# Modulated-convolution chain on one core: third output sum placed in PSUM, blurred taps built on TensorE, tap combinations and both ends reordered

## The chip, the cores and the metric

One core of a Trainium2 chip. The time is the device time of one execution in microseconds, data already in the chip's memory. Three runs of the kernel before took 515.73, 516.54 and 517.63 us; the median, 516.54 us, is the number to be compared. One further execution was taken with the hardware profiler; its own time is 515.94 us. All data are float32.

## The reference

Each of 128 samples has 64 channels and 1024 positions. A style vector of the sample gives each of four convolution layers a scale per input channel; the scaled weights are normalised per output channel; the four layers run one after the other and the input is added at the end:

```python
def _layer(x, style, w, b, mw, mb, typ):
    s = style @ mw.T + mb
    weight = SCALE * w * s[:, None, :, None]
    demod = lax.rsqrt(jnp.sum(weight * weight, axis=(2, 3)) + EPS)
    weight = weight * demod[:, :, None, None]
    ...                      # conv with 3 taps, + b
    # 'upsample': transposed conv of stride 2, then a blur (1,3,3,1)
    # 'downsample': the blur, then a conv of stride 2
...
for i, typ in enumerate(('same', 'upsample', 'same', 'downsample')):
    out = _layer(out, style, weights[i], biases[i], mod_w[i], mod_b[i], typ)
return x + out
```

There is no nonlinearity between the layers, so for each sample the whole chain is one filter of 9 taps of 64x64 matrices (different near the two ends of the sequence) and one constant per output channel.

## The kernel before, in words

**Filters.** Samples go in pairs (64 pairs p; one sample of the pair in partitions 0 to 63, one in 64 to 127) and the filters in quads of four samples (32 quads q, two pairs each). A quad's filter comes from three stages of matmuls, each followed by copies that multiply by a per-sample scale: `stage1` (matmuls L306, copies into S by L284 on ScalarE or L286 on VectorE), `stage2` (L337, copies into R), and `stage3` in two parts (L374, copies into Wf). `scale3` makes the scaled last-layer weights that stage 1 starts from. `stage2` multiplies S by E, the 9 taps of the upsampling layer with the two blurs already folded in (the seven factors of `BLUR2` over 3 taps). E is made once, near the start: VectorE clears it and `blur` adds seven scaled copies of the layer's weights (L275), in three portions that the written order spreads over the start. Then `residual` (L404) adds the input's own contribution to the centre tap, and `combine` (L412 to L416, five VectorE instructions of 384 columns) forms three sums of taps, H1, H2 and H3.

**Convolution.** The positions of a sample are split into three phases, positions 3j, 3j+1 and 3j+2, so that three outputs y0, y1, y2 of 170 columns each come from five products of filters of three taps instead of nine. The five inputs T of a pair are sums and differences of the phases: `pre1` makes G (L440, L443 on VectorE) and two of the five (L447, L448 on POOL), `pre2a` (L453) and `pre2b` (L463) the other three. `pre1` and `pre2a` also issue, on SP's queue, the loads of the pair four on. `convA12` computes the products with H1 and H2, `convA3` that with H3, into a PSUM tile psA; ScalarE copies m1 (L506) and m3 (L519, L520) to SBUF. `seed1` forms u and v (L528, L529), `seed2` adds u and m3 into Y (L547) and puts y1 = 2 m3 + v into SBUF (L548). Y is a PSUM tile of 512 columns for each of the pair's two samples, one bank each. `convB` accumulates the two last products onto Y's blocks 0 and 1 (matmuls at L481, as those of `convA`). `output` multiplies each sample's result by a scale and adds the constant: with ScalarE (L572) or VectorE (L574), one instruction of 340 columns from Y and one of 170 from y1. `store` sends the sample out, on SP's queue (L577). There is one Y for all pairs but a few at the end (`Y2`, two more banks, pairs 60 and 62).

**What sets the order.** Nothing is scheduled automatically: each engine executes its instructions in the order in which the program is written. The main loop, one pass for each quad, writes: stage 2 of quad q+2, `convB` and the outputs of pair 2q, stage 3 of quad q+2, `convA12` of pair 2q+2, inputs, stores, the seeds of pair 2q+1, `convA3`, then the same for pair 2q+1, stage 1 of quad q+3, and the combinations of quad q+2. Two tables put side work into it (`EXTRA` on VectorE and POOL, `SLOTS` on TensorE): constants, the normalisers of the later samples, and the few columns at both ends of the sequences. Samples are prepared in three parts (`PART`: 0 to 15, 16 to 31, the rest). The start (L816 to L898) is written out by hand: it computes the scales of part 0, makes the tables tA, tB, tC, t0, t3 that the stages multiply by, fills waiting time on TensorE with multiplications by zero (`zeros_to_y`), computes the constants of part 0 (`const_first`, `const_rest`; the last of them gives oc, which the outputs add) and works through quads 0 and 1 and pairs 0 to 2 until the loop can take over. `var_inverse`, `var_newton`, `table_A` and `table_C` turn a part's variances into its normalisers and tables, the first two on VectorE, the tables on POOL. The last two passes (q = 30, 31) have orders of their own; the last pair's outputs are written block by block, alternately on ScalarE and VectorE.

The code below has the line numbers of the profile.

## Time and profile before

| | |
|---|---|
| median of 3 runs | 516.54 us (515.73 to 517.63) |
| the profiled execution | 515.94 us |
| its span, first to last instruction | 514.1 us |
| TensorE, matmuls and weight loads | 492.9 us and 467.9 us busy (96% and 91%) |
| VectorE | 476.7 us (93%) |
| ScalarE | 364.0 us (71%) |
| POOL (GpSimd) | 159.7 us (31%) |
| mean granted clock of TensorE | 0.993 |
| DMA | 70.91 MB, 138 GB/s over the span |
| L547, the seed sum into Y | 62 times, mean 1083 ns |
| L548, y1 into SBUF | 64 times, mean 940 ns |
| L572, outputs on ScalarE | 340 columns and a few of 170: 126 times, mean 633 ns; 170 columns from y1: 125 times, mean 526 ns |

How the profile is read: PE is TensorE's matmuls and PEld its weight loads, which overlap; DVE is VectorE, ACT ScalarE, SP the engine whose queue issues loads and stores. A group of instructions is named by its line, its engine and what it writes and reads (`Y<-u,m` reads u and m and writes Y). Matmuls of 64x64 on different quarters of TensorE overlap (the 4608 of `convA` have a mean of 304 ns, and 193.9 us busy together), so a group's busy time is less than number times mean. A wait is written with the waiting instruction, then what released it (`PEld Y L481 <- DVE Y L547` is a weight load of `convB` that waited for the seed sum), the total in us, how often, and the longest. In rows in order of time, a bracket at the end holds the idle time before that instruction and what ended it.

### The profile page before, as it was taken

Reading aid. Unit: us, or ns where it says so; the run is one execution under the profiler, and the core shown is the slowest. Engines: PE = TensorE matmul, PEld = TensorE weight load, DVE = VectorE, ACT = ScalarE, POOL = GpSimd, SP = SyncE. Lnnn points to the kernel's source line nnn. Section 1 sums busy time; section 2 is a strip of 40 time slices with the busy share of each in tenths; the row PEclk is TensorE's granted clock in tenths of the full one; section 3 lists DMA queues with packets and bytes.
Section 4 is the critical chain, followed back from the end, with each engine's and each line's share of the span. In section 5 each row is a group of like instructions: output and inputs, shape, how many; then the busy total and the mean of one; then the engine's idle time right before and its main releaser. Section 6 shows DMA issues by size and latency. Waiting matters only on the chain.

```text
span 514.1 us, 28399 instructions
## 1 busy us (share of the span) xinstructions
PE 492.9 (96%) x12612; PEld 467.9 (91%) x12612; DVE 476.7 (93%) x869; ACT 364.0 (71%) x908; POOL 159.7 (31%) x196
## 2 busy tenths in 40 slices
PE   8998699998999999999999999999999999999994
PEld 5997699998899989999999999889999999999983
DVE  6899989999999999999989999989999979999994
ACT  3466567776766877777877777777777768777753
POOL 3315633443423331322221332331333213322210
PEclk9999999999999999999999999999999999999998
DMA  7125544553434544544554454554555435543223
GB/s 253 44 70 159 162 128 126 167 152 103 145 117 155 166 133 125 159 131 126 166 155 128 136 140 122 160 154 129 138 164 153 149 118 173 154 137 126 84 86 123
DMA packets 37162, 70.91 MB, mean 138 GB/s; under 512 B 4144, under 2 KB 28464, under 8 KB 37040
## 3 DMA queue, kind: packets, MB, share of 16 engines
q1 hardware_dynamic: 36960, 68.85, 44.3%
q8 instruction: 99, 1.62, 1.4%
q10 hardware_dynamic: 80, 0.25, 0.1%
q14 instruction: 23, 0.19, 0.1%
HBM read 35.46 MB, written 33.62 MB: 134 GB/s over the span
## 4 chain that ended last, share of the span: by engine, by line
PE 65%; DVE 20%; ACT 3%; issue 2%; DVEq 0%
PE psA L481 21%; PE Y L481 18%; PE psR L337 11%; PE psW L374 9%; PE psS L306 4%; DVE Y L547 3%; DVE T L463 3%; DVE y L548 2%; DVE G L440 2%; PE psE L724 2%; ACT o L572 2%; DVE G L443 1%; DVE u L528 1%; DVE T L453 1%; DVE H L413 1%
## 5 line engine op out<-in xcount | busy, mean ns | idle before, releaser
L481 PE MATMUL psA<-T,H 64*64 64x170 f32 x4608 | 193.9, 304 | 1.0 <-DVE v L529 1.0
L481 PEld LDWEIGHTS psA<-T,H 64*64 64x64 f32 x4608 | 176.9, 133 | 2.2 <-issue 1.6
L447 POOL TENSOR_TENSOR T<-G 128x342 f32<-128x342 f32 x62 | 57.0, 920 | 312.8 <-DVE G L443 266.7
L481 PE MATMUL Y<-T,Wf 64*64 64x170 f32 x3072 | 131.3, 307 | 12.0 <-DVE Y L547 10.9
L481 PEld LDWEIGHTS Y<-T,Wf 64*64 64x64 f32 x3072 | 115.9, 133 | 18.0 <-DVE Y L547 15.0
L572 ACT ACTIVATE o<-Y,oc,dm 128x340 f32<-128x340 f32 (+1 forms) x126 | 79.8, 633 | 48.0 <-PE Y L481 47.2
L374 PE MATMUL psW<-R,par_oi 64*64 64x256 f32 (+3 forms) x1536 | 92.4, 350 | 0.0
L284 ACT ACTIVATE Wf<-psW,t 128x256 f32<-128x256 f32 (+1 forms) x252 | 75.3, 381 | 22.5 <-PE psW L374 22.2
L337 PE MATMUL psR<-S,E 64*64 64x192 f32 (+1 forms) x2304 | 89.7, 299 | 0.2 <-ACT S L284 0.2
L547 DVE TENSOR_TENSOR Y<-u,m 128x680 f32<-128x680 f32 x62 | 67.2, 1083 | 17.2 <-ACT o L572 17.0
L337 PEld LDWEIGHTS psR<-S,E 64*64 64x64 f32 x2304 | 81.6, 133 | 1.7 <-ACT S L284 0.7
L448 POOL TENSOR_TENSOR T<-G 128x342 f32<-128x342 f32 x62 | 82.0, 1323 | 0.0
L374 PEld LDWEIGHTS psW<-R,par_oi 64*64 64x64 f32 x1536 | 73.2, 133 | 8.0 <-PE Y L643 0.3
L572 ACT ACTIVATE o<-y,oc,dm 128x170 f32<-128x170 f32 x125 | 65.8, 526 | 0.3 <-DVE y L548 0.3
L284 ACT ACTIVATE R<-psR,tC 128x448 f32<-128x448 f32 x63 | 36.5, 630 | 40.5 <-PE psR L337 40.5
L548 DVE SCALAR_TENSOR_TENSOR y<-m,v 128x340 f32<-128x340 f32 x64 | 60.2, 940 | 0.0
L440 DVE SCALAR_TENSOR_TENSOR G<-X 128x688 f32<-128x688 f32 x64 | 56.4, 882 | 0.0
L463 DVE TENSOR_TENSOR T<-G 128x684 f32<-128x684 f32 x64 | 56.3, 881 | 0.0
L306 PE MATMUL psS<-wd,par_oi 64*64 64x192 f32 x768 | 40.3, 324 | 0.0
L506 ACT ACTIVATE m<-psA 128x340 f32<-128x340 f32 x64 | 29.3, 458 | 10.4 <-PE psA L481 7.6
L306 PEld LDWEIGHTS psS<-wd,par_oi 64*64 64x64 f32 x768 | 32.2, 133 | 1.4 <-ACT wd L284 0.5
L528 DVE SCALAR_TENSOR_TENSOR u<-psA,m 128x340 f32<-128x340 f32 x64 | 32.1, 502 | 0.8 <-ACT m L520 0.8
(127 smaller groups left out, 446.1 us busy)
## 6 DMA issues: line engine op xcount, KB each, us to landing
out<-o SPq DMA_DIRECT2D x128, 255.0 KB, 3.6
X<-in_x SPq DMA_DIRECT2D x60, 344.0 KB, 3.2
X<-in_x SPq DMA_DIRECT2D x60, 172.0 KB, 3.5
X<-in_x SPq DMA_DIRECT2D x4, 516.0 KB, 6.5
Xe<-in_x_ends SPq DMA_DIRECT2D x1, 512.0 KB, 4.0
par_oi<-in_params_oi SPq DMA_DIRECT2D x2, 208.0 KB, 4.9
par_io<-in_params_io ACTq DMA_DIRECT2D x1, 240.0 KB, 3.8
par_io<-in_params_io SPq DMA_DIRECT2D x1, 240.0 KB, 4.4
```

The costliest lines, as they stand in the source:

```text
L284: nc_a.activation(dst, src, AF.Copy, scale=f)
L306: nc.tensor.matmul(ps[r][cols, k * C : (k + K) * C], woi[rows, 2, k, :], src[rows, :], start=(k == 0), stop=(k == K - 1), skip_group_check ...
L337: nc.tensor.matmul(ps[r][cols, lo * C : (lo + m) * C], E[rows, e + 2, :], src[rows, a, :], start=(n == 0), stop=(n == 8), skip_group_check ...
L374: nc.tensor.matmul(ps[r][cols, (lo - t_lo) * C : (hi - t_lo) * C], woi[rows, 0, k, :], rt[c][rows, lo - k : hi - k, :], start=(k == order[0]),
L440: nc_v.scalar_tensor_tensor(g[:, PL:], X[:, : 2 * PL], 0.5, X[:, PL:], op0=ALU.mult, op1=ALU.subtract)
L447: eng.tensor_add(t[:, 2, :NJ], plane(g, 2), plane(g, 1))
L448: eng.tensor_sub(t[:, 3, :NJ], plane(g, 2), plane(g, 1))
L463: nc_v.tensor_sub(t[:, 0:2, :NJ], both(a, PL), both(b, 1))
L481: nc.tensor.matmul(ps[s][cols], w, Ts[p][rows, SLOT[m], j : j + NB], start=(g == 0 and m not in (0, 4)), stop=(g == 2), skip_group_check=True,
L547: nc_v.tensor_add(blocks(Y), uu, m3)
L548: nc_v.scalar_tensor_tensor(y1, m3[:, :, 0, :], 2.0, v, op0=ALU.mult, op1=ALU.add)
L572: nc_a.activation(dst, src, AF.Identity, bias=add, scale=d3)
```

## The change

y1 is written into columns 340 to 509 of Y, beside the sums that `convB` accumulates on, and the output of a sample is one instruction of 510 columns from Y. E is made by TensorE: ScalarE makes four scaled copies of the layer's weights, 28 matmuls with the identity add them up in Y, one VectorE and one ScalarE copy bring them to E, whose taps are now stored even ones first. The combinations follow another order, with `residual` in their midst. At the start, the zero multiplications go partly to other banks; stage 1 of quad 0, the inputs of pair 0 (`pre1(0)`) and the last constant of part 0 come earlier, the normalisers of part 1 later, in the first pass of the loop behind the seeds of pair 1, and pair 0's stores both ahead of them. At the end, the pass q = 30 makes the last pair's inputs after the seeds of pair 61, its `convA3` right behind its `convA12`, and the first half of its seeds early; its outputs are all read from Y.

The diff; lines of code that only changed place are marked as removed and added.

```diff
     one = const.tile([P, 1], F32, name="one")
     eps = const.tile([P, 1], F32, name="eps")
     Z = const.tile([P, 512], F32, name="Z")
     E = const.tile([P, NT, C], F32, name="E")
+    w1s = const.tile([P, K + 1, K, C], F32, name="w1s")
     nc_v.memset(one, 1.0)
     nc_v.memset(Z, 0.0)
-    nc_v.memset(E, 0.0)
     nc_v.memset(eps, EPS)
 
     nc_a.activation(one, one, AF.Sqrt)
...
         table(nc_g, t3, bs, ALT, ODD, dm[:, 3, bs], var[:, 3, bs])
 
 
-    def blur(i, j):
-        for b in range(i, j):
-            dst = E[:, b : b + K, :]
-            nc_v.scalar_tensor_tensor(dst, w1r, BLUR2[b], dst, op0=ALU.mult, op1=ALU.add)
+    def blur_scale():
+        for i in range(K + 1):
+            nc_a.activation(w1s[:, i], w1r, AF.Copy, scale=BLUR2[i])
+
+    def blur_matmul(ps):
+
+        for b in range(len(BLUR2)):
+            w = w1s[:, min(b, len(BLUR2) - 1 - b)]
+            for r, rows in enumerate(HALF):
+
+                both = b % 2 == r
+                src = w[rows, 0::2] if both else w[rows, 1]
+                at = (b if both else b + 1) // 2
+                for cols in HALF:
+                    nc.tensor.matmul(
+                        ps[r][cols, C * at : C * (at + 1 + both)],
+                        idn[rows],
+                        src,
+                        start=(b == 0),
+                        stop=(b == len(BLUR2) - 1),
+                        skip_group_check=True,
+                    )
+
+    def blur_copy(ps, engs):
+        for r, (i, j) in enumerate(((0, 5), (5, NT))):
+            dst, src = E[:, i:j].rearrange("c e i -> c (e i)"), ps[r][:, : (j - i) * C]
+            if engs[r] is nc_a:
+                nc_a.copy(dst, src)
+            else:
+                engs[r].tensor_copy(dst, src)
 
 
     w3 = wio[:, 3]
...
                     src = st[c if r == 0 else 1 - c]
                     nc.tensor.matmul(
                         ps[r][cols, lo * C : (lo + m) * C],
-                        E[rows, e + 2, :],
+                        E[rows, e // 2 + 1 + (e % 2) * 5, :],
                         src[rows, a, :],
                         start=(n == 0),
                         stop=(n == 8),
...
         h1, h2, h3 = (H_[:, i] for i in range(3))
 
         nc_v.scalar_tensor_tensor(h2, c, -0.5, a, op0=ALU.mult, op1=ALU.add)
+        residual(q)
+        nc_v.scalar_tensor_tensor(h3, c, -1.5, h2, op0=ALU.mult, op1=ALU.add)
         nc_v.tensor_add(h1, h2, b)
         nc_v.tensor_sub(h2, h2, b)
-        nc_v.scalar_tensor_tensor(h3, c, -1.5, h2, op0=ALU.mult, op1=ALU.add)
-        nc_v.scalar_tensor_tensor(h3, b, 3.0, h3, op0=ALU.mult, op1=ALU.add)
+        nc_v.scalar_tensor_tensor(h3, b, 2.0, h3, op0=ALU.mult, op1=ALU.add)
 
 
     NJ = 2 * NB + 2
...
         nc_v.scalar_tensor_tensor(v, m2, 1.0 / 3.0, m1, op0=ALU.mult, op1=ALU.add)
         part[p] = m3, u, v
 
-    y1s = {}
-
     def seed2(p):
         if p >= NP:
             return
         m3, u, v = part.pop(p)
-        y1s[p] = y1 = m_tile("y1", p)
         uu = u[:, :, None, :].to_broadcast([P, 2, 2, NB])
         blocks = lambda y: y[..., : 2 * NB].rearrange("c s (i j) -> c s i j", i=2)
+        y1 = slice(2 * NB, 3 * NB)
         if p in Y2:
-            for s in range(2):
-                nc_v.tensor_add(
-                    blocks(y_bank(p, s)[:, None, :]), uu[:, s : s + 1], m3[:, s : s + 1]
-                )
+            ys = [(y_bank(p, s)[:, None, :], slice(s, s + 1)) for s in range(2)]
         else:
-            nc_v.tensor_add(blocks(Y), uu, m3)
-        nc_v.scalar_tensor_tensor(y1, m3[:, :, 0, :], 2.0, v, op0=ALU.mult, op1=ALU.add)
+            ys = [(Y, slice(0, 2))]
+        for y, k in ys:
+            nc_v.tensor_add(blocks(y), uu[:, k], m3[:, k])
+        for y, k in ys:
+            nc_v.scalar_tensor_tensor(
+                y[..., y1], m3[:, k, 0, :], 2.0, v[:, k], op0=ALU.mult, op1=ALU.add
+            )
 
     def seed(p):
         seed1(p)
...
         Ts.pop(p)
         os[p] = opool.tile([P, 2, HO], F32, tag="o", name=f"o{p}")
 
-    def output(p, s, eng=nc_a, parts=((0, 2), (2, 3))):
+    def output(p, s, eng=nc_a, parts=((0, 3),)):
 
         b = 2 * p + s
         d3, add = dm[:, 3, b : b + 1], oc[:, b : b + 1]
         for i, j in parts:
             dst = os[p][:, s, i * NB : j * NB]
-            src = y1s[p][:, s] if i == 2 else y_bank(p, s)[:, i * NB : j * NB]
+            src = y_bank(p, s)[:, i * NB : j * NB]
             if eng is nc_a:
                 nc_a.activation(dst, src, AF.Identity, bias=add, scale=d3)
             else:
...
     pm = [unit(ps_conv, f"psM{i}") for i in range(2)]
     BOTH = nc_a, nc_v
     LATER = slice(PART[0].stop, B)
+    Y2["fill"] = unit(ps_w, "psF")
     n_later = NL * (B - PART[0].stop)
     zeros_to_y(2, 512)
     nc_v.tensor_scalar_mul(mbs, mb, SCALE)
     mod_matmul(PART[0], pm[0][0])
     nc_a.activation(wsq[T, :2], wio[T, :2], AF.Square)
     nc_v.tensor_mul(wsq[T, 2:], wio[T, 2:], wio[T, 2:])
+    blur_scale()
     zeros_to_y(4, 256)
     mod_scale(PART[0], pm[0][0])
     nc_v.tensor_add(q2[T], wsq[T, :, 0, :], wsq[T, :, 1, :])
...
     for table_of in (table_B, table_0, table_02):
         table_of(PART[0])
     var_matmul(PART[0], pm[0][1])
-    blur(0, 1)
     var_root(PART[0], pm[0][1])
+    psB = [Y[:, r] for r in range(2)]
+    blur_matmul(psB)
     mod_matmul(LATER, pm[1][0])
 
-    zeros_to_y(4, 256)
+    zeros_to_y(2, 256, "fill")
     weight_sums()
     first_inverse(PART[0])
     table_A(PART[0], d2)
     scale3(0, BOTH)
+    blur_copy(psB, BOTH)
+    stage1(0, None, BOTH)
     scale3(1)
     nc_a.copy(raw[0][:, 0, :n_later], pm[1][0][:, :n_later])
-    blur(1, 3)
     var_inverse(PART[0])
     var_newton(PART[0])
     for of in (table_C, vector_c0, table_3, vector_a1, vector_Da, vector_b1, vector_c2):
         of(PART[0])
-    stage1(0, None, BOTH)
     scale3(2)
     zeros_to_y(2, 256)
-    blur(3, 7)
+    pre1(0, nc_v)
     mod_scale(PART[1], raw[0][:, 0], LATER)
     for of in (table_B, vector_a1, table_0, table_02, vector_b1, vector_c2):
         of(PART[1])
     stage2(0, None, BOTH)
-    pre1(0, nc_v)
     pre2a(0)
     zeros_to_y(2, 512)
     const_first(0, PART[0])
...
     stage3(0, 1, None, BOTH)
     stage1(2, ps_conv)
     const_first(2, PART[0])
-    residual(0)
     combine(0)
+    const_rest(2, PART[0], const_of(2, PART[0]))
     stage2(1, ps_conv)
     convA12(0)
     convA3(0)
...
     convA12(1)
     stage3(1, 1)
     convA3(1)
-    const_rest(2, PART[0], const_of(2, PART[0]))
-    residual(1)
     combine(1)
     pre2a(2)
     seed1(1)
     pre2b(1)
     pre1(3)
-    var_inverse(PART[1])
-    var_newton(PART[1])
-    table_A(PART[1], dm[:, 2, PART[1]])
-    for of in (table_C, vector_c0, table_3, vector_Da):
-        of(PART[1])
 
 
     REST = PART[2]
...
         if c < NQ:
             stage3(c, 0)
         if q == NQ - 1:
-            seed(p + 1)
+            seed2(p + 1)
         output(p, 1, nc_a if q < NQ - 1 else nc_v)
         if q == NQ - 1:
             store(p, 0)
...
         convA12(p + 2)
 
         if q:
-            pre2(p + 3)
+            if q < NQ - 2:
+                pre2(p + 3)
             store(p, 0)
             pre1(p + 4)
             store(p, 1)
             seed(p + 1)
+            if q == NQ - 2:
+                pre2(p + 3)
         else:
             store(p, 0)
+            store(p, 1)
             seed2(p + 1)
+            var_inverse(PART[1])
+            var_newton(PART[1])
+            table_A(PART[1], dm[:, 2, PART[1]])
+            for of in (table_C, vector_c0, table_3, vector_Da):
+                of(PART[1])
             pre2(p + 3)
-            store(p, 1)
             pre2b(p + 2)
             pre1(p + 4)
         EXTRA.get((q, 0), lambda: None)()
...
         convA3(p + 2)
         if q == NQ - 2:
             convA12(p + 3)
+            convA3(p + 3)
         side = SLOTS.get(q)
         convB(p + 1, (lambda: slot(*side)) if side else None)
         if q == NQ - 2:
             seed(p + 2)
+            seed1(p + 3)
         output(p + 1, 0)
         output(p + 1, 1, nc_a if q < NQ - 2 else nc_v)
         if c == NQ - 1:
...
         if s + 1 < NQ:
             scale3(s + 1)
         if c < NQ:
-            residual(c)
-            combine(c)
+                combine(c)
         EXTRA.get((q, 1), lambda: None)()
         if q < NQ - 2:
             convA12(p + 3)
-        convA3(p + 3)
+            convA3(p + 3)
 
 
 def kernel(x, cond_512, L0_cond_weights, L0_cond_biases, L0_cond_mod_w, L0_cond_mod_b):
```

## The prediction

> **What bounds the kernel now.** I read the page first, then the waits, then the timeline pair by pair. Engines first (busy us, share of the span, instructions):
>
> ```profile
> span 514.1 us, 28399 instructions
> PE 492.9 (96%) x12612; PEld 467.9 (91%) x12612; DVE 476.7 (93%) x869; ACT 364.0 (71%) x908; POOL 159.7 (31%) x196
> ```
>
> TensorE and VectorE are both nearly full, so neither share says which sets the end. The waits do (us in total, times, longest):
>
> ```profile
> DVE Y L547 <- ACT o L572: 17.0, 19, 3.0
> PEld Y L481 <- DVE Y L547: 15.0, 14, 3.1
> ...
> PE Y L481 <- DVE Y L547: 10.9, 10, 2.8
> ```
>
> The bound alternates. In some pairs `convB` waits for VectorE's seed L547 (VectorE leads); in others L547 waits for ScalarE's outputs, which follow TensorE (TensorE leads). Going through the 64 pairs in the timeline, VectorE leads in pairs 1 to 3, 6 to 19, 22 to 25, 32 to 39, and briefly at 43 and 53; TensorE in the rest. Pair 35, led by VectorE (start us, us):
>
> ```profile
> 306.32 0.92 POOL L447 TENSOR_TENSOR T<-G 128x342 f32<-128x342 f32 x1 [6.19 <-DVE G L443]
> ...
> 306.91 1.06 DVE L547 TENSOR_TENSOR Y<-u,m 128x680 f32<-128x680 f32 x1
> 307.19 1.54 POOL L448 TENSOR_TENSOR T<-G 128x342 f32<-128x342 f32 x1
> ...
> 307.88 1.22 DVE L548 SCALAR_TENSOR_TENSOR y<-m,v 128x340 f32<-128x340 f32 x1
> 308.02 1.65 PEld L481 LDWEIGHTS Y<-T,Wf 64*64 64x64 f32 x48 [0.75 <-DVE Y L547]
> ```
>
> TensorE starts 0.05 us after L547 ends (307.97), while L548 (y1) still runs: y1 is off TensorE's path today. L548 takes 1.22 us here and 0.50 elsewhere: L448 holds it up until 308.73, and 0.4 later it ends.
>
> **y1 to PSUM.** The instruction stays, one L548 per pair. No row shows this form writing PSUM; L547 (680 elements to PSUM) and L463 (684 to SBUF) both take 0.86 us undisturbed, so I take no change. Bounds 0 and +0.1 us each: it now waits for the instruction just ahead of it, which elsewhere costs VectorE 0.11 us; where L448 is in the way, that is hidden.
>
> Does its collision with POOL go, now that it no longer writes SBUF? The row first: L548 loses 0.72 us beside L448, while L528 and L529 lose nothing beside L447 (0.50 us); those read one operand from PSUM. The Trainium skill (SBUF — State Buffer, "SBUF: two separate sides") says that a VectorE instruction with two SBUF inputs and a GpSimd instruction that reads SBUF shut each other out for the whole instruction. It names inputs, not the output, and y1's inputs m3 and v stay in SBUF. If the write mattered, some 40 contended L548 would shed 0.72 us each, 29 us of VectorE time; by the rule nothing. I take nothing.
>
> What changes is who waits. y1 now lies in the bank that `convB` accumulates in. The row above says that `convB` needs L547 alone: cost 0. The Trainium skill (PSUM — Partial Sum Buffer, "PSUM bank collisions raise a hardware error") says that two engines may not touch one bank and quadrant together even at different columns, so waits go by bank. The built program does that: in every pair the first `convB` matmul waits for the y1 instruction instead of the seed sum. By the row 0; by the rule 1.08 us (y1's end less today's start) where VectorE leads. I take the rule. Queued behind that matmul on TensorE are the rest of `convB` and stages 1 to 3; ScalarE's outputs and the next L547 wait for those. For a pair's second `convB` y1 ends 0.7 to 2 us before TensorE comes: nothing there.
>
> Within a VectorE-led stretch this is a shift, not a sum. At pair 11 the outputs free Y at 128.88 and the next L547 starts at 129.97: 1.09 us of cover. One output of 510 columns replaces 340 and 170: ScalarE's rows from 64 to 448 columns rise 0.82 ns per column (315 to 630 ns), so 636+140=776 ns, 0.67 from start to start against 0.96 for the two; Y frees 0.15 us sooner. So the cover just holds. But each handover from VectorE to TensorE pays 1.08-0.15 once; without the cover, every pair of a stretch would pay it.
>
> **Combinations reordered.** One block today:
>
> ```profile
> 300.42 0.47 DVE L404 SCALAR_TENSOR_TENSOR Wf<-par_oi,t,Wf 128x64 f32<-128x64 f32 x2
> 300.81 0.54 DVE L412 SCALAR_TENSOR_TENSOR H<-Wf 128x384 f32<-128x384 f32 x1
> 301.39 0.56 DVE L413 TENSOR_TENSOR H<-H,Wf 128x384 f32<-128x384 f32 x1
> ...
> 303.17 0.56 DVE L416 SCALAR_TENSOR_TENSOR H<-Wf,H 128x384 f32<-128x384 f32 x1
> 303.65 0.51 DVE L453 TENSOR_TENSOR T<-X 128x342 f32<-128x342 f32 x1
> ```
>
> Each of the five steps needs the one before: 0.59 from start to start; the independent L453 follows after 0.48. Today 3.23 us. After, one dependent neighbour is left: four at 0.48, one at 0.59, two residuals at 0.2: 2.91. That saves 0.32 us per two pairs, on the path only where VectorE leads: seven times in pairs 6 to 19. h1 comes 0.4 us later; `convA12` comes 1.6 us after it, which covers that.
>
> **Start.** Off VectorE: the memset of E (0.48) and seven blur steps (7 x 0.36=2.5). Onto it: one PSUM copy (256 columns; L286 has 0.54 for 320: 0.45). Onto ScalarE: four copies of 192 (0.38 each, in its 2.4 us wait for the variance matmuls) and one of 320 (0.53). Onto TensorE: 28 short matmuls ahead of stage 1, for 4 zero matmuls less: 0 to 0.7 us, I take 0.3. VectorE is idle 3.5 us between 5 and 25, so the 2.5 are not simply won. And `pre1(0)` (2.2 us, 15.76 to 17.96) now stands ahead of VectorE's half of R: S ends at 12.0, Newton 1.3, `pre1(0)` 2.2, sc and ssq 0.5: R at 16.0+0.3, not 15.15. Stage 3 begins 1.2 later; behind it the waits for constants (0.41+0.34) go, as VectorE is ready then: +0.5 at the first u (28.05).
>
> From u on VectorE is full to pair 2 (51.71). The oc instructions leave this stretch (1.03 us, 31.31 to 32.34), combine(1) saves 0.3 but waits 0.5 for Wf: 0.5-1.0-0.3+0.5=-0.3. The inverses of part 1 (2.7 us, 39.68 to 42.38) move behind the second seed: `convB(1)`, which waits 2.12 us today, starts some 1.2 earlier, but those 2.7 us then stand ahead of pair 2, whose L547 gains 0.3 only. With y1, `convB(2)` is 0.8 later, `convB(3)` 0.5. POOL's tables follow the inverses later, and their readers (quad 4 on) come later still. SP's queue takes pair 0's second store ahead of two loads; they feed pairs four on. Behind pair 3 the clock matters (columns: width, busy us of PE, PEld, DVE, ACT, POOL; granted clock; DMA):
>
> ```profile
> 60.00:62.00 2.00, 0.00 (x0) 0.00 (x0) 2.00 (x5) 0.95 (x3) 1.29 (x2) 1.00 0.98 290
> 62.00:64.00 2.00, 1.59 (x30) 1.54 (x32) 2.00 (x4) 0.00 (x0) 1.93 (x3) 0.76 0.71 213
> 64.00:66.00 2.00, 2.00 (x34) 2.00 (x34) 2.00 (x4) 0.55 (x2) 1.92 (x3) 0.50 0.35 92
> 66.00:68.00 2.00, 2.00 (x54) 2.00 (x50) 1.21 (x3) 1.12 (x3) 1.08 (x3) 0.89 0.25 96
> ```
>
> After some 3 us without matmuls the clock halves for 3.4 us: 1.7 us lost, where TensorE leads. In the new order it is idle about 3.3 us before `convB(2)`, where VectorE's lead hides a slow clock, and 2.7 before `convB(3)`. Bounds 0 and -1.7; I take half, -0.85. At pair 5: -0.4.
>
> **Middle.** Pairs 6 to 19: 1.08-7x0.32-0.15=-1.3. Pairs 22 to 25, two savings only: +0.6. Pairs 32 to 39, with four and their own slack: 0. At 43 and 53: +0.6 and +0.4. In ten first halves led by TensorE y1 (0.50) ends 0 to 0.4 after `convB` starts today; POOL, released earlier, gives some back: +0.7. Sum +1.0.
>
> **End.** seed(61) now precedes pre2(63), so `convA12(63)` loses its 0.99 us wait, but its `convA3`, drawn ahead, waits 0.5 for m1's copy: the last matmul ends 0.5 sooner. Then:
>
> ```profile
> 508.06 0.49 ACT L572 ACTIVATE o<-Y,oc,dm 128x170 f32<-128x170 f32 x1 [1.19 <-PE Y L481]
> 508.59 0.45 DVE L574 TENSOR_SCALAR o<-Y,dm,oc 128x170 f32<-128x170 f32 x1 [1.18 <-ACT o L572]
> 509.08 0.49 ACT L572 ACTIVATE o<-Y,oc,dm 128x170 f32<-128x170 f32 x1 [0.52 <-DVE o L574]
> 509.60 0.45 DVE L574 TENSOR_SCALAR o<-Y,dm,oc 128x170 f32<-128x170 f32 x1 [0.56 <-ACT o L572]
> ```
>
> Four outputs, 0.51 apart, follow the last matmul in turn. The third block came from SBUF during `convB`; now it is in Y and joins them: six in turn, +1.0. End +0.5.
>
> **Sum.** -0.4+1.0+0.5=+1.1. The profiled execution took 515.94 us (514.1 span, 1.8 around it): 517.0. The median of the runs is 0.6 above it: 517.6.
>
> **Rivals.** (1) Slower: the wait for y1 is not won back. `convB` behind y1 at the ends of five VectorE-led stretches, 5 x 0.93=4.7, and 0.5 at the end: 521.7. For it: the built waits, and TensorE's start 0.05 after L547. It decides if the reorder saves under some 0.15 us per block; against that, 0.11 us per dependent step in the rows. (2) Faster: VectorE's relief reaches the end. 16 blocks at 0.32 are 5.1, within the 10.9 us that TensorE waits, and if y1 slips from behind POOL (0.50) the new wait is free: 511.4. For it: pairs 26 to 31, where y1 has 0.50. Against: in VectorE-led pairs POOL starts right after L443. (3) The start keeps the 2.5 us that leave VectorE, and the clock stays full: 513.0. Against: `pre1(0)` ahead of R.
>
> **How the numbers follow.** Near the old time 0.5; rival 1 0.3; rival 2 0.12; rival 3 0.08. A measurement of this kernel tells about 0.5% (2.6 us) from no change. The first case's own range is 515 to 520.5; 0.05 of it lies above 519.1, and half of rival 3 within the bound. Faster 0.17, same 0.49, slower 0.34. The range 512.6 to 522 cuts rival 2 and the tail of rival 1.
>
> **What would show it.** `convB`'s waits name y1; y1's median stays near 1.2 us; the block takes 2.9 us; outputs of 510 columns 0.78 us; six outputs in turn at the end; stage 3 of quad 0 about 1 us later. The forecast is wrong if y1 falls to 0.5 us throughout, if the clock drops in more places, or if the seeds no longer wait for outputs anywhere.

## The result, and the profile after

The changed kernel takes 525.46 us (four runs, 523.97 to 526.51) against 517.09 us for the kernel before (four runs, 515.73 to 518.06): 1.0162 times as long, 95% interval 1.0126 to 1.0197. The forecast was 517.6, with a range up to 522.0. The profiled execution took 525.72 us with a span of 523.9, against 514.1.

The page after, its first lines and the groups that answer to those of before (busy us, mean ns, then idle time before them and its releaser):

```profile
span 523.9 us, 28402 instructions
...
PE 499.4 (95%) x12660; PEld 471.0 (90%) x12660; DVE 458.5 (88%) x862; ACT 332.1 (63%) x789; POOL 150.0 (29%) x196
...
L509 PE MATMUL Y<-T,Wf 64*64 64x170 f32 x3072 | 129.8, 308 | 14.3 <-DVE Y L574 11.3
...
L600 ACT ACTIVATE o<-Y,oc,dm 128x510 f32<-128x510 f32 (+1 forms) x127 | 95.0, 773 | 54.1 <-PE Y L509 51.1
L572 DVE TENSOR_TENSOR Y<-u,m 128x680 f32<-128x680 f32 (+1 forms) x66 | 72.3, 1099 | 38.9 <-ACT o L600 38.7
...
L574 DVE SCALAR_TENSOR_TENSOR Y<-m,v 128x340 f32<-128x340 f32 (+1 forms) x66 | 45.4, 690 | 2.1
```

VectorE's busy time fell from 476.7 to 458.5 us and ScalarE's from 364.0 to 332.1, and the kernel became slower: less work, more waiting. The waits (us in total, times, longest):

```profile
DVE Y L572 <- ACT o L600: 38.7, 39, 3.2
...
PE Y L509 <- DVE Y L574: 11.3, 11, 3.6
...
PEld Y L509 <- DVE Y L574: 4.3, 2, 4.0
```

VectorE's seed sum now waits for ScalarE's outputs for 38.7 us in 39 places, not 17.0 in 19. Where `convB` waits for VectorE, it waits for y1 (L574), not for the sum, as forecast. (The profile puts another 10.9 us of waits ahead of `convB` down to ScalarE's copies into Wf. In the first halves looked at below those copies aren't what releases it: `convB` begins between 0.07 and 0.66 us after the last of them that had ended, but 0.14 or 0.15 us after y1 in every case.)

The chain behind this is seen in the timeline. This is the first half of one pass in which VectorE has slack, from the first `convB` to the second (start us, us, engine, line, what it writes and reads, count; in brackets the idle time before it and what ended it):

```profile
460.09 1.95 PE L509 MATMUL Y<-T,Wf 64*64 64x170 f32 x48
...
461.82 1.51 PE L401 MATMUL psW<-R,par_oi 64*64 64x320 f32 x24
462.10 0.78 ACT L600 ACTIVATE o<-Y,oc,dm 128x510 f32<-128x510 f32 x1 [0.60 <-PE Y L509]
...
463.36 1.25 ACT L311 ACTIVATE Wf<-psW,t 128x256 f32<-128x256 f32 x4 [0.48 <-PE psW L401]
...
464.11 0.93 POOL L476 TENSOR_TENSOR T<-G 128x342 f32<-128x342 f32 x1
464.48 0.79 ACT L600 ACTIVATE o<-Y,oc,dm 128x510 f32<-128x510 f32 x1
...
465.31 0.88 DVE L572 TENSOR_TENSOR Y<-u,m 128x680 f32<-128x680 f32 x1 [1.40 <-ACT o L600]
...
465.82 1.08 PE L509 MATMUL psA<-T,H 64*64 64x170 f32 x24
...
466.22 0.52 DVE L574 SCALAR_TENSOR_TENSOR Y<-m,v 128x340 f32<-128x340 f32 x1
...
466.89 1.39 PE L509 MATMUL Y<-T,Wf 64*64 64x170 f32 x32
```

Read it by who waits. ScalarE's first output (462.10) follows `convB`; then, by the written order, come stage 3's four copies (463.36), which wait for stage 3's matmuls; only then the second sample's output (464.48). It frees Y at 465.27, 5.18 us after `convB` began. The sum starts at 465.31, y1 behind it, and y1 ends at 466.74, 6.65 us after. The second `convB` begins at 466.89, 6.80 after. TensorE's own work between the two takes 6.59 us, as other runs below show. So even in this quiet pass the chain is 0.2 us too long; 0.15 of it is the longer output (y1_odd below, which has outputs of 340 and 170 columns again ahead of this sum, has 6.65 us here instead of 6.80). In a pass with side work on VectorE, POOL comes later and stands beside the sum:

```profile
325.26 0.80 ACT L600 ACTIVATE o<-Y,oc,dm 128x510 f32<-128x510 f32 x1
...
325.91 0.91 POOL L476 TENSOR_TENSOR T<-G 128x342 f32<-128x342 f32 x1
...
326.08 1.47 DVE L572 TENSOR_TENSOR Y<-u,m 128x680 f32<-128x680 f32 x1 [0.38 <-ACT o L600]
...
327.59 0.52 DVE L574 SCALAR_TENSOR_TENSOR Y<-m,v 128x340 f32<-128x340 f32 x1
```

Here the sum takes 1.47 us instead of 0.88, beside L476 on POOL, and the chain grows by as much: from `convB` at 320.87 to the next at 328.25 are 7.38 us. Such passes carry most of the loss. Against y1_sbuf (below; y1 in SBUF, the rest as in the change), the 25 first halves of q = 4 to 28 are 8.6 us longer together. Eight of them, in which the sum or y1 runs longer beside POOL, make 5.3 of that, at 0.3 to 0.9 each; fifteen make 3.3, at 0.2 to 0.3 each; two, led by VectorE in both kernels, lose nothing.

With all kernels of the study side by side (from their profiled executions; pass by pass for q = 4 to 28), the loss in the main loop lies in these first halves and nowhere else. What each kernel changes is told below; the columns from the fourth on are in us, but for the count:

| kernel | median us | ratio to before (95%) | `convB` of pair 5 begins | pair 5 to pair 59 | first half, mean | of 25 first halves below 6.62 us | second half, mean |
|---|---|---|---|---|---|---|---|
| before | 517.09 | | 79.2 | 408.6 | 6.93 | 11 | 8.26 |
| the change | 525.46 | 1.0162 (1.0126 to 1.0197) | 82.2 | 413.9 | 7.09 | 0 | 8.26 |
| y1_only | 532.22 | 1.0285 (1.0252 to 1.0318) | 82.2 | 418.7 | 7.28 | 0 | 8.26 |
| y1_sbuf | 511.63 | 0.9899 (0.9869 to 0.9929) | 79.3 | 404.2 | 6.75 | 16 | 8.25 |
| comb_only | 510.50 | 0.9880 (0.9851 to 0.9909) | 81.4 | 403.4 | 6.73 | 16 | 8.25 |
| old_start | 523.42 | 1.0131 (1.0099 to 1.0164) | 79.8 | 413.9 | 7.09 | 0 | 8.25 |
| out_early | 517.06 | 0.9988 (0.9975 to 1.0001) | 80.6 | 407.3 | 6.86 | 12 | 8.25 |
| out_early_sbuf | 519.55 | 1.0037 (1.0023 to 1.0050) | 78.9 | 412.4 | 7.05 | 0 | 8.25 |
| y1_first_sbuf | 513.75 | 0.9914 (0.9894 to 0.9933) | 81.3 | 405.2 | 6.79 | 16 | 8.25 |
| sbuf_oldblur | 512.20 | 0.9887 (0.9870 to 0.9905) | 81.1 | 404.2 | 6.75 | 16 | 8.25 |
| y1_even | 512.61 | 0.9913 (0.9889 to 0.9938) | 81.1 | 403.9 | 6.73 | 16 | 8.26 |
| y1_odd | 523.63 | 1.0113 (1.0076 to 1.0150) | 83.7 | 411.1 | 7.00 | 0 | 8.25 |
| comb_q0 | 508.73 | 0.9836 (0.9812 to 0.9860) | 77.3 | 404.1 | 6.75 | 17 | 8.25 |
| comb_q0_blur | 510.29 | 0.9865 (0.9813 to 0.9916) | 79.7 | 403.9 | 6.75 | 16 | 8.25 |

### The profile page after: what moved, and what is told of

The parts are those of the page before. It is cut to its first block, busy times and chain, and to the rows that moved or that the text cites. A ratio compares the mean times of both kernels' runs of the same rounds, so it can differ in the third digit from the quotient of the medians.

```text
span 523.9 us, 28402 instructions
## 1 busy us (share of the span) xinstructions
PE 499.4 (95%) x12660; PEld 471.0 (90%) x12660; DVE 458.5 (88%) x862; ACT 332.1 (63%) x789; POOL 150.0 (29%) x196
## 4 chain that ended last, share of the span: by engine, by line
PE 74%; DVE 11%; ACT 4%; issue 1%; DVEq 0%
PE psA L509 24%; PE Y L509 21%; PE psR L364 12%; PE psW L401 10%; PE psS L333 5%; DVE Y L572 3%; PE psE L752 2%; ACT Wf L311 2%; DVE Y L574 2%; ACT o L600 1%; DVE T L491 1%; DVE G L468 1%; DVE G L471 1%; DVE o L602 0%; DVE u L556 0%
## 5 line engine op out<-in xcount | busy, mean ns | idle before, releaser
L509 PE MATMUL psA<-T,H 64*64 64x170 f32 x4608 | 190.1, 304 | 0.7 <-ACT m L534 0.6
L509 PEld LDWEIGHTS psA<-T,H 64*64 64x64 f32 x4608 | 173.4, 133 | 1.7 <-ACT m L534 0.9
L475 POOL TENSOR_TENSOR T<-G 128x342 f32<-128x342 f32 x62 | 57.1, 920 | 325.7 <-DVE G L471 265.0
L509 PE MATMUL Y<-T,Wf 64*64 64x170 f32 x3072 | 129.8, 308 | 14.3 <-DVE Y L574 11.3
L509 PEld LDWEIGHTS Y<-T,Wf 64*64 64x64 f32 x3072 | 113.6, 134 | 24.6 <-ACT Wf L311 10.9
L600 ACT ACTIVATE o<-Y,oc,dm 128x510 f32<-128x510 f32 (+1 forms) x127 | 95.0, 773 | 54.1 <-PE Y L509 51.1
L572 DVE TENSOR_TENSOR Y<-u,m 128x680 f32<-128x680 f32 (+1 forms) x66 | 72.3, 1099 | 38.9 <-ACT o L600 38.7
L401 PE MATMUL psW<-R,par_oi 64*64 64x256 f32 (+3 forms) x1536 | 90.1, 350 | 0.2 <-DVE R L313 0.2
L476 POOL TENSOR_TENSOR T<-G 128x342 f32<-128x342 f32 x62 | 70.8, 1142 | 0.0
L574 DVE SCALAR_TENSOR_TENSOR Y<-m,v 128x340 f32<-128x340 f32 (+1 forms) x66 | 45.4, 690 | 2.1
L311 ACT ACTIVATE S<-psS,tB 128x320 f32<-128x320 f32 x63 | 29.8, 530 | 5.3 <-PE psS L333 3.9
```

Of the source, the lines that this page charges most:

```text
L311: nc_a.activation(dst, src, AF.Copy, scale=f)
L401: nc.tensor.matmul(ps[r][cols, (lo - t_lo) * C : (hi - t_lo) * C], woi[rows, 0, k, :], rt[c][rows, lo - k : hi - k, :], start=(k == order[0]),
L475: eng.tensor_add(t[:, 2, :NJ], plane(g, 2), plane(g, 1))
L476: eng.tensor_sub(t[:, 3, :NJ], plane(g, 2), plane(g, 1))
L509: nc.tensor.matmul(ps[s][cols], w, Ts[p][rows, SLOT[m], j : j + NB], start=(g == 0 and m not in (0, 4)), stop=(g == 2), skip_group_check=True,
L572: nc_v.tensor_add(blocks(y), uu[:, k], m3[:, k])
```

## The experiments

**y1 in PSUM alone, and undone.** Into the kernel before went only the changed `seed2` and `output`:

```diff
-        nc_v.scalar_tensor_tensor(y1, m3[:, :, 0, :], 2.0, v, op0=ALU.mult, op1=ALU.add)
+        for y, k in ys:
+            nc_v.scalar_tensor_tensor(
+                y[..., y1], m3[:, k, 0, :], 2.0, v[:, k], op0=ALU.mult, op1=ALU.add
+            )
...
-    def output(p, s, eng=nc_a, parts=((0, 2), (2, 3))):
+    def output(p, s, eng=nc_a, parts=((0, 3),)):
```

> The kernel before with one part alone: y1 goes to PSUM and each sample's output is one instruction (third block from Y at the end too). Theory 1 (one Y, a longer chain from one convB to the next): in TensorE-led passes convA3 of the first half is followed by convB after 1.06 us, not 0.87, in others after up to 1.8; passes 12 to 30 lose some 5 us, the VectorE-led passes before them some 2 more since the reordered combinations don't help here, the tail loses 1.0: 523 to 525 us. Theory 2 (y1 in PSUM is harmless, the middle loses by the reordered combinations and by collisions with POOL): at most 519 us.

It took 532.22 us, worse than either theory said. (In this kernel, and in old_start below, y1 of pair 0 overwrites the columns of Y from which the last constant of the first 16 samples is read afterwards, so that constant isn't the reference's; the instructions are the same.) The same edit reversed in the changed kernel:

> The changed kernel with that part undone: y1 in SBUF again, two outputs for each sample. Theory 1: the step from convA3 to convB is 0.87 us again in TensorE-led passes, 5 us come back in the middle and 1.0 in the tail: 519 to 520 us, 2.7 of the rest from the start. Theory 2: no more than 2 us come back, 523 us or more.

It took 511.63 us, faster than the kernel before. So y1 in PSUM costs 13.8 us (525.46 less 511.63) beside the reordered combinations, and 15.1 (532.22 less 517.09) without them. By place, from the profiles of the change and of y1_sbuf, which lie 14.9 us apart: 2.9 us before pair 5, 9.7 from there to pair 59, 2.3 behind it. (Of the 2.9, 1.3 lie ahead of pair 0's `convB`, where the two kernels do the same: that is a difference between two executions, see the start below.) Theory 2 falls. That more came than theory 1 said has one reason: I had read the cost off the change against the kernel before, where the gain of another part hid it.

**The combinations alone.**

```diff
-        nc_v.tensor_add(h1, h2, b)
-        nc_v.tensor_sub(h2, h2, b)
-        nc_v.scalar_tensor_tensor(h3, c, -1.5, h2, op0=ALU.mult, op1=ALU.add)
-        nc_v.scalar_tensor_tensor(h3, b, 3.0, h3, op0=ALU.mult, op1=ALU.add)
+        residual(q)
+        nc_v.scalar_tensor_tensor(h3, c, -1.5, h2, op0=ALU.mult, op1=ALU.add)
+        nc_v.tensor_add(h1, h2, b)
+        nc_v.tensor_sub(h2, h2, b)
+        nc_v.scalar_tensor_tensor(h3, b, 2.0, h3, op0=ALU.mult, op1=ALU.add)
```

> The kernel before with the reordered combinations alone. Theory 1: 0.3 us saved on VectorE in each block; it reaches the end where VectorE leads, about eight blocks, 1 to 2.5 us: 514.5 to 516 us. Theory 2 (h1 and h3 come later, TensorE waits for them): 518 us or more.

510.50 us: 6.6 us gained, more than twice what was expected. The block went from 3.23 to 2.85 us from start to start, in 30 blocks. First halves at TensorE's own pace, 6.59 us, are 16 of 25 instead of 11: VectorE's lead, which came and went in the kernel before, is gone in five more of them, and the others are shorter too (the 25 together by 5.0 us).

**Where y1's cost sits: the second output ahead of stage 3.** If the chain is what costs, it must help to let ScalarE free Y before stage 3's copies:

```diff
         output(p, 0)
+        if q < NQ - 1:
+            output(p, 1)
         if c < NQ:
             stage3(c, 0)
...
-        output(p, 1, nc_a if q < NQ - 1 else nc_v)
```

> The changed kernel with one edit: in the first half of a pass the second sample's output is written ahead of stage 3, so that ScalarE frees Y before it scales stage 3's first part, not after. Theory 1 (the cost of y1 in PSUM is the length of the chain convB, stage 3's copies, second output, seed sum, y1, next convB): the chain is 1.1 us shorter, below TensorE's own 6.6 us; convA3 is followed by convB after 0.87 us again, passes take 14.39 us, 8 to 10 us come back: 516 to 518 us. Theory 3 (the cost lies in y1's write itself, VectorE and TensorE in one bank, or in collisions with POOL): the wait stays, 523 us or more.

517.06 us: 8.4 us came back, as theory 1 said; theory 3 falls. (5.4 us over y1_sbuf remain, 3.1 of them in the loop. Of these, 2.4 lie in four first halves in which Y is free 3.4 to 3.6 us after `convB` began, but VectorE comes to the sum only at 4.8 to 5.2.) The same stretch as above, in this kernel:

```profile
453.70 0.75 PE L509 MATMUL Y<-T,Wf 64*64 64x170 f32 x14
...
454.51 1.44 ACT L600 ACTIVATE o<-Y,oc,dm 128x510 f32<-128x510 f32 x2 [0.60 <-PE Y L509]
...
455.84 1.24 ACT L311 ACTIVATE Wf<-psW,t 128x256 f32<-128x256 f32 x4
...
456.32 1.06 DVE L572 TENSOR_TENSOR Y<-u,m 128x680 f32<-128x680 f32 x1
...
457.29 1.16 PE L401 MATMUL psW<-R,par_oi 64*64 64x256 f32 x24
457.42 1.12 DVE L574 SCALAR_TENSOR_TENSOR Y<-m,v 128x340 f32<-128x340 f32 x1
...
458.26 1.05 PE L509 MATMUL psA<-T,H 64*64 64x170 f32 x24
...
459.12 1.17 PE L509 MATMUL Y<-T,Wf 64*64 64x170 f32 x25
```

Both outputs end at 455.95. The sum now waits for VectorE itself, y1 ends at 458.54, and `convB` begins at 459.12, right behind the third product: 6.59 us after the one before. The sum and y1 are both slower here than in the change (1.06 and 1.12, not 0.88 and 0.52) and yet cost nothing. In this pass the pace is set by the length of the chain, not by the price of y1.

The same edit where y1 is in SBUF:

> The undone run (y1 in SBUF) with the second sample's output ahead of stage 3. Theory 1: its passes are at TensorE's 14.39 us already, so little is left to win: 510.5 to 511.6 us. A rival (stage 3's copies, now later, hold up its second part): 513 us or more.

519.55 us, 7.9 us worse: the rival was right. Four outputs are now ahead of stage 3's copies:

```profile
456.91 0.63 ACT L600 ACTIVATE o<-Y,oc,dm 128x340 f32<-128x340 f32 x1 [0.86 <-PE Y L509]
...
457.44 0.52 ACT L600 ACTIVATE o<-y,oc,dm 128x170 f32<-128x170 f32 x1
...
457.87 0.62 ACT L600 ACTIVATE o<-Y,oc,dm 128x340 f32<-128x340 f32 x1
...
458.38 0.52 ACT L600 ACTIVATE o<-y,oc,dm 128x170 f32<-128x170 f32 x1
...
458.81 1.24 ACT L311 ACTIVATE Wf<-psW,t 128x256 f32<-128x256 f32 x4
...
459.52 0.43 PE L401 MATMUL psW<-R,par_oi 64*64 64x256 f32 x2
...
460.09 0.62 PEld L401 LDWEIGHTS psW<-R,par_oi 64*64 64x64 f32 x16 [0.38 <-ACT Wf L311]
```

They hold ScalarE for 1.9 us (456.91 to 458.81), where the two of 510 columns hold it for 1.3 (454.51 to 455.84); only then come the copies, and stage 3's second part needs the PSUM tiles that they empty: its weight load at 460.09 has waited 0.38 us for them. Every first half pays: 7.05 us in the mean, none at 6.59. An order that wins in one version loses in the other.

**y1 ahead of the sum, in SBUF.**

```diff
+        nc_v.scalar_tensor_tensor(y1, m3[:, :, 0, :], 2.0, v, op0=ALU.mult, op1=ALU.add)
...
             nc_v.tensor_add(blocks(Y), uu, m3)
-        nc_v.scalar_tensor_tensor(y1, m3[:, :, 0, :], 2.0, v, op0=ALU.mult, op1=ALU.add)
```

> y1 in SBUF and two outputs for each sample, as in the run with that part undone, but y1 is computed ahead of the seed sum, so that convB waits for both as it does in the changed kernel, with no bank shared. Theory 1: the sum comes 0.45 us later, 1.2 where POOL is in y1's way; Y is freed as early as in the undone run (340 columns, 0.14 us sooner than 510), so a part of the 14 us comes, 3 to 8: 514.5 to 519.5 us. Theory 3 (the bank, not the order): as the undone run, 511.6 us.

513.75 us, 2.1 over y1_sbuf, where theory 1 had named 3 to 8, and of it only 1.0 in the loop. The reason is in the undone kernel's timeline:

```profile
452.52 0.65 ACT L600 ACTIVATE o<-Y,oc,dm 128x340 f32<-128x340 f32 x1
...
453.04 0.55 ACT L600 ACTIVATE o<-y,oc,dm 128x170 f32<-128x170 f32 x1
453.21 0.88 DVE L575 TENSOR_TENSOR Y<-u,m 128x680 f32<-128x680 f32 x1 [0.98 <-ACT o L600]
...
454.00 0.50 DVE L576 SCALAR_TENSOR_TENSOR y<-m,v 128x340 f32<-128x340 f32 x1
454.00 1.02 PE L509 MATMUL psA<-T,H 64*64 64x170 f32 x21
...
454.76 0.32 PE L509 MATMUL Y<-T,Wf 64*64 64x170 f32 x2
```

VectorE has stood idle for 0.98 us before the sum, waiting for Y. A y1 that goes to SBUF fits into that gap: in the same pass of y1_first_sbuf, y1 runs from 454.70 to 455.28, and VectorE then still waits 0.95 us, until the sum starts at 456.23. A y1 that goes to Y can't start until Y is free. This is the part of theory 1 that I had missed: it isn't that `convB` waits for y1, but that y1 itself waits for the outputs.

**Which pairs.** y1 in PSUM for even pairs only, and for odd pairs only (`in_psum` is `p % 2 == 0` or `p % 2 == 1`):

```diff
             ys = [(Y, slice(0, 2))]
+        if not in_psum(p):
+            y1s[p] = m_tile("y1", p)
...
+        if p in y1s and parts == ((0, 3),):
+            parts = (0, 2), (2, 3)
```

> The changed kernel with y1 in PSUM, and one output for each sample, for even pairs only; odd pairs have y1 in SBUF and two outputs. Theory 1 (the chain from a pass's first convB to its second is the one without slack; the sum of an even pair is ready 2 us early): convA3 is followed by convB after 0.87 us, the even pairs' longer outputs use 0.17 of a slack of 0.67, passes take 14.39 us: 511.5 to 513 us. Rival (every y1 in PSUM costs its share): about half of the 14 us, 517 to 519 us.

> The reverse: y1 in PSUM for odd pairs (and for the two pairs that use the second Y), in SBUF for the other even pairs. Theory 1: the chain of a first half is 5.04 to the sum, 0.88, y1 0.56 and 0.14 to convB, 6.62 us against TensorE's 6.59, so quiet passes lose nothing and those where POOL collides with the sum or y1 lose 0.6: some 3 to 6 us over y1 in SBUF, 514.5 to 518 us, and more than the even pairs cost. Rival: as the even pairs, 517 to 519 us.

Even pairs: 512.61 us, 1.0 over y1_sbuf, none of it in the loop (403.9 against 404.2). Odd pairs: 523.63, 12.0 over it, 6.8 of them in the loop (411.1). The place is as theory 1 says; the size of the second was missed. Quiet first halves take 6.65 us there, as expected, but the other 16 of 25 are longer by 0.06 to 1.1 us, where VectorE is late or POOL stands beside the sum or y1; I had counted too few of them.

**The start.** The old blur and order in the changed kernel, from the first instruction to the end of the first pass:

```diff
-    blur_scale()
...
+    blur(0, 1)
     var_root(PART[0], pm[0][1])
-    psB = [Y[:, r] for r in range(2)]
-    blur_matmul(psB)
...
-    blur_copy(psB, BOTH)
-    stage1(0, None, BOTH)
...
+    blur(1, 3)
...
+    stage1(0, None, BOTH)
...
+    blur(3, 7)
-    pre1(0, nc_v)
...
```

> The changed kernel with the old start: E made on VectorE, the old written order up to the loop and in its first pass. Theory 1 (the blurred taps put 2.6 us of TensorE ahead of stage 1 of quad 0, and nothing later wins them back, since from pass 12 on TensorE leads): stage 1 of quad 0 begins at 9.9 us instead of 12.8, the result is 2 to 3 us below the changed kernel, 522.5 to 523.5 us. Rival: the slack of the VectorE-led passes 4 to 11 absorbs the start, less than 1 us comes back, 525 us.

523.42 us, 2.0 less than the change, at the edge of what four runs each tell apart (523.0 to 525.4 against 524.0 to 526.5); from pair 5 on the two run alike (413.9). The total is in theory 1's range, but not its reason: stage 1 of quad 0 begins at 11.39 us, not at 9.9, so only 1.45 us sooner than in the change (12.84). Why the 9.9 of the kernel before didn't come again is told at the end of this section.

Next, y1_sbuf with the old blur alone, the new order kept:

> The undone run (y1 in SBUF, the new orders at both ends) with E made on VectorE as before. Theory 1: stage 1 of quad 0 begins at 9.9 us instead of 12.8, and the 2.6 us of blur matmuls go; VectorE takes 2.5 us more, partly in its gaps: 1 to 2.5 us less than the undone run, 509 to 510.5 us. Rival: VectorE's extra steps stand in its way as long, 511.6 us.

512.20 us against 511.63: no gain, a miss. In the new order the seven blur steps stand on VectorE ahead of pair 0's inputs and of R; that they are the reason isn't shown, since the two profiles also differ in TensorE's pace up to 14 us (see the end of this section).

Of the new start, added to comb_only, the moves around the first pass alone:

```diff
     combine(0)
+    const_rest(2, PART[0], const_of(2, PART[0]))
...
-    const_rest(2, PART[0], const_of(2, PART[0]))
...
-    var_inverse(PART[1])
-    var_newton(PART[1])
...
             store(p, 0)
+            store(p, 1)
             seed2(p + 1)
+            var_inverse(PART[1])
+            var_newton(PART[1])
...
             pre2(p + 3)
-            store(p, 1)
```

> The kernel before with the reordered combinations, and of the new start only this: the last constant of part 0 earlier, part 1's inverses and both stores of pair 0 moved as in the change. Theory: convB of pair 1 starts 1.5 us or more sooner, but the inverses stand ahead of pair 2, so 510 to 511.5 us, as the combinations alone; the 1 us that the undone run lies above them is then the blur on TensorE and pair 0's inputs. Rival: this move is what costs it, 511.5 us or more.

508.73 us, 1.8 less than the combinations alone and 8.4 less than the kernel before: the fastest of all. `convB` of pair 1 begins 6.6 us after that of pair 0, not 8.8, but pair 2 17.9 after, not 18.2: the inverses take nearly all of it back, as expected. The rest shows behind pair 3, in the stretch at half clock: it lasts from 62 to 70 us in the profile of comb_only and from 52 to 56 in this one, and costs TensorE 3.4 us there and 1.7 here (granted clock 0.72, 0.50, 0.50 and 0.58 in four stretches of 2 us; 0.61 and 0.54 in two). (The profiled execution of comb_only, 512.09 us at a mean granted clock of 0.990, was the slowest of its four; the other three took 510.2 to 510.8 us at 0.994 and 0.995, so the longer stretch isn't usual for it.) How much of the 1.8 is the order's and how much the clock's stays open. To this the blur on TensorE was added alone:

```diff
+    blur_scale()
...
-    blur(0, 1)
     var_root(PART[0], pm[0][1])
+    psB = [Y[:, r] for r in range(2)]
+    blur_matmul(psB)
...
-    zeros_to_y(4, 256)
+    zeros_to_y(2, 256, "fill")
...
     scale3(0, BOTH)
+    blur_copy(psB, BOTH)
     scale3(1)
...
-    blur(1, 3)
...
-    blur(3, 7)
```

> The kernel with the reordered combinations and the moved constants and inverses, and E made on TensorE as in the change, with the rest of the start in its old order. Theory (28 matmuls of E take 2.6 us of TensorE ahead of stage 1 of quad 0, against 2 zero fills less, 0.6, and 2.5 us less on VectorE, which is partly idle there): stage 1 some 1 to 1.5 us later, 509.5 to 511 us against 508.7. Rival (the blur on TensorE is hidden, and what remains of the start's cost is pair 0's inputs ahead of R): 508.7 us.

510.29 us, 1.6 more; the two intervals overlap, so the total alone doesn't settle it. Part of the 1.6 may be the clock's again: the four executions fall with it (512.66 us at a mean of 0.990, 511.08 at 0.992, 509.44 and 509.50 at 0.994), and in the profile of this kernel the half clock lasts from 54 to 61 us. The profiles do settle the place: from the first input's use to the first matmul of stage 1 of quad 0 it is 9.29 us (3.89 to 13.18), against 7.43 (3.31 to 10.74). The row in the change, and what stands around it on TensorE:

```profile
4.59 1.99 PE L169 MATMUL Y<-Z 64*64 64x256 f32 x16
...
7.34 2.60 PE L287 MATMUL Y<-w1s,par_oi 64*64 64x128 f32 x56
9.87 1.76 PE L188 MATMUL psM<-par_s 128*64 128x112 f32 x16
11.56 1.13 PE L169 MATMUL psF<-Z 64*64 64x256 f32 x8
12.84 1.43 PE L333 MATMUL psS<-wd,par_oi 64*64 64x192 f32 x24
14.08 0.62 PE L169 MATMUL Y<-Z 64*64 64x256 f32 x8
```

28 matmuls (each is two records here) take 2.60 us, 93 ns each, with nothing beside them. But TensorE is not yet at its full pace there: eight records of zero fills take 1.13 us at 11.56 and 0.62 at 14.08. The kernel before shows the same turn, only earlier:

```profile
4.70 1.99 PE L168 MATMUL Y<-Z 64*64 64x256 f32 x16
...
8.78 1.09 PE L168 MATMUL Y<-Z 64*64 64x256 f32 x16
```

The granted clock reads 1.00 over this whole stretch, but the traces hold no record of the clock until 8.42 us in the profile of before and 13.35 us in that of the change, and it is there that the pace rises; in the other twelve profiles it does so between 10.2 and 14.0 us. So the profile of before, from which I forecast the start, was an early one: y1_only and comb_only, with the same start, begin stage 1 at 11.21 and 11.49 us, not at 9.91. The 28 matmuls fell into the slow time in all eight profiles that have them. At its pace (1.99 us for 16 records of 256 columns) their 5376 columns come to the 2.6 us measured; at the later one (1.09 us) to an estimated 1.4.

## Why the prediction was wrong

The built waits were read rightly. Rival 1, which named them, had the sign and the wait right, but it placed the cost at the ends of five stretches led by VectorE, and its 521.7 was too low. By the steps of the prediction:

- *The bound alternates.* Right for the kernel before. Wrong in what I took from it: that pairs led by TensorE have room. In a first half they have 0.67 us (y1_sbuf: sum ended at 454.09, `convB` began at 454.76), and y1 in PSUM needs more.
- *y1's own time.* Right: 0.52 us where POOL is away (0.50 before) and 1.11 beside POOL (1.22 before). The collision with POOL stayed, with 0.11 us less of it; the rule weighed there (two SBUF inputs, whatever the output) held against the hope that writing PSUM would end it. That y1's median would stay near 1.2 was wrong: it is 0.52, since only 20 of 66 now meet POOL, not 39 of 64.
- *Waits go by bank.* Right. `convB` began 0.14 or 0.15 us after y1 ended in each of the 25 first halves.
- *A shift, not a sum.* **This is the step that failed.** I charged y1 once at each of five handovers from VectorE to TensorE, and +0.7 for ten first halves led by TensorE together. With 13 blocks saved at 0.32 (4.2) that made +1.0 for the middle, so 5.2 for y1. (For pairs 22 to 25 the terms that I named, 1.08-0.15-2x0.32, give 0.3, not the 0.6 that I put in.) Measured from pair 5 to pair 59, the change is +5.3, and y1 costs 9.7 there. It is a sum: each of the 27 passes in between has a first half in which Y must be freed, seeded twice and only then used, and each one that TensorE leads pays what the chain is over 6.59 us. None of it is won back later: the second halves take 8.26 us in the change and 8.25 in y1_sbuf. I looked at the cover in front of the sum in a pass led by VectorE, and never added up the chain of a pass led by TensorE.
- *Y frees 0.15 us sooner.* Right for two outputs behind each other (1.44 us until Y is free in out_early, 1.58 in out_early_sbuf; the second halves, where they stand so, lose nothing). Wrong in first halves: there the two samples' outputs are apart, stage 3's copies lie between, and the sum waited for the 340 columns alone, since y1's 170 came from elsewhere. The single output ends 5.18 us after `convB`, not 5.01: 0.17 later.
- *Combinations.* Mechanism right, 2.91 us a block forecast, 2.85 measured. The worth was mis-sized: 4.2 us in 13 blocks where VectorE leads; alone it brings 6.6, 5.2 of them from pair 5 to pair 59. Rival 2's sum, 5.1, was near that; that rival erred in letting y1 go free.
- *Start.* -0.4 us in all was forecast, and y1's 0.8 is in that, so about -1.2 for the start itself; +2.0 was measured (the change less old_start, both with y1 in PSUM), at the edge of the noise. The mis-sized term is the 28 matmuls: 0.3 us for them less four zero matmuls, where they took 2.60 and the four (eight records at half pace, 1.0) gave back less than half. I called them short, where a row was near: the zero fills at 4.70 in the profile of before, 1.99 us for 4096 columns, make 2.6 for their 5376. The moved constants and inverses had -0.3 at pair 2, and the profiles show that (17.9 for 18.2); in the total they brought 1.8, with the clock's part of it open. The half clock came back, near 58 us instead of 64, and for 3.4 us in both profiles: it was no shorter.
- *End.* The six outputs in turn: from the start of the first to the end of the last 3.03 us (516.71 to 519.74), against 1.99: +1.0, as forecast. The last matmul 0.5 us sooner did not come. From `convB` of pair 60 to it are 15.25 us before and 15.38 in the change, but 14.78 in y1_sbuf, with the same order at the end, and 14.69 in comb_only, with the old one: the combinations gain this, the order at the end does not, and y1 takes it back.

Together: y1 +13.8 (the change less y1_sbuf), combinations -6.6 (comb_only less before) and the rest of the start and the end +1.1 (y1_sbuf less comb_only). These are steps from one kernel to the next, so that they add up to the 8.4 us measured by themselves; in another order the steps differ somewhat (y1 alone, without the new combinations, was 15.1). The forecast had about +7.0 for y1 (5.2 in the middle, 0.8 at the start, 1.0 in the tail), -4.2, and -1.7 for what is left of its +1.1. Of the 7.3 us between the two, y1 is 6.8. The start and the end came 2.8 dearer than forecast and the combinations 2.4 cheaper, which nearly cancels.

What stays open beside the clock: y1_sbuf (511.63) differs from comb_q0_blur (510.29) in pair 0's inputs and stage 1 being earlier and in the order at the end; the intervals overlap, and neither was tried alone. The end is not it: from `convB` of pair 59 to the last instruction are 25.5 us in y1_sbuf and 25.7 in comb_q0_blur.

## What to carry to other kernels

Where one buffer is freed, filled and used in turn, add up that chain from use to use for the bound's own pass, and compare it with the bound's work in between, before pricing any one instruction on it: here an instruction was free below it, and each pass paid in full above it. The write into the shared PSUM bank cost more here than the wait behind it: it could not start before the outputs had freed the bank (VectorE idle for 1.40 us in the quiet pass), where the same result in SBUF filled that idle time. And price a saving in every place where its engine could come to lead, not only where it leads now.

## What the runs showed of the hardware

- Beside POOL's L476, y1 took 1.11 us to PSUM and 1.22 us to SBUF, 0.52 and 0.50 alone: the destination hardly mattered.
- TensorE began at about half pace, where the granted clock of the profile reads 1.00: 16 records of 256 columns took 1.99 us, at 4.4 to 5.5 us from the start, in all 14 profiles, and 1.09 behind the turn in that of before. The same 16 matmuls (the scales of the later samples) took 1.76 us ahead of the turn, and 1.47 (before) or 1.21 (y1_sbuf) across it. The turn came between 10.2 and 13.4 us in seven profiles that share the change's start, and the first input came to use between 3.31 and 4.50 us: the start of one execution can't be read to better than about 1 us against another's.
- A stretch at half clock of 3.4 us, in four kernels of 6.8 (in y1_only and y1_odd two of 3.4), stands between 45 and 71 us in every one of the 14 profiles (63.0 to 66.4 before, 57.7 to 61.1 in the change, 62.9 to 69.7 in comb_only), in or shortly after an idle time of TensorE of 2.0 to 4.9 us. Not every such idle time has one: 2.5 us in old_start (61.9 to 64.4) was followed by none.
